# Two banks in turn for a layer's first groups, weight folding on four row groups with three buffers, and another order of tiles

## The chip, the cores and the metric

The kernel runs on one core of one Trainium2 chip. The metric is the device time of one execution in microseconds; of several executions the median is given. The engines are TensorE (PE in the profile, its weight loads PEld), VectorE (DVE), ScalarE (ACT), GpSimd (POOL) and SyncE (SP); all five take their instructions in order, each from its own queue, and wait for each other by semaphores. DMA transfers are issued here by SP and POOL, and each transfer's end is a semaphore event as well.

## The reference

A batch of 1024 images of 16 x 16 with 16 channels, in fp32, goes through four layers. Each computes `x = x + f(groupnorm(x))` with 8 groups of two channels.

```python
def _tt_matvec(vector, cores):          # layer 0: a 4096 x 4096 matrix as a train of three cores
    res = vector[:, None]
    for core in cores:
        r, o, i, k = core.shape
        res_t = res.reshape(bs, r, i, -1)
        new = jnp.einsum('roik,brix->bkox', core, res_t)
        ...

def update(x):                          # layers 1 and 3
    xt = jnp.transpose(x, (0, 3, 2, 1))
    pre = _alive(xt)                    # 3x3 maximum of channel 3 over 0.1
    y1 = _depthwise(xt, conv1_w, conv1_b)
    y2 = _depthwise(xt, conv2_w, conv2_b)
    p = jnp.concatenate([xt, y1, y2], axis=1)
    h = jax.nn.relu(p.reshape(B * W * Hh, 48) @ fc0_w.T + fc0_b)
    d = (h @ fc1_w.T + fc1_b).reshape(B, C, W, Hh)
    xn = (xt + d) * (pre & _alive(d)).astype(xn.dtype)
    ...

def _L2_conv_ref(x, filters, bias):     # layer 2: 3x3 convolution, 16 to 16 channels
    ...

x = x + _L0_conv_ref(_gn(x), ...)
x = x + _L1_conv_ref(_gn(x), ...)
x = x + _L2_conv_ref(_gn(x), ...)
x = x + _L3_conv_ref(_gn(x), ...)
```

## The kernel before, in words

**Data.** The batch is two chunks of 512 images (NB). The free dimension of nearly all tiles is the 512 images of a chunk; lines of an image stand on the 128 partitions. Two buffers, `XN[0]` and `XN[1]`, hold the chunk that is worked on and the one that is prepared.

**Layer 0 (`layer_train`).** The train of cores is multiplied out on the chip: `train_setup` computes G, the product of two cores (`gs`, eight groups of four matmuls for each half of the input, evacuated by ACT at L554 and sent to memory), and `build(u)` multiplies G with the third core to the weights of one unit: eight matmuls on four row groups of 32 partitions (L1009) into four PSUM banks of tag "w", four copies by ACT (L1014), and sums by DVE (`mix`, L1027). The 4096 x 4096 product itself is done by seven products in the manner of Strassen, over the two chunks as one of its dimensions. It has five phases with 16 units each; a unit of phase 0 has two products, of phase 1 five, and of the others seven, each product being four matmuls of 512 columns (L1086). PSUM for this layer has eight banks: three with tag "o" for products, four with tag "w" for builds, and a single one with tag "m" for everything else.

**What lies beside the products.** The order of every engine is written by hand: `run(layer, us, loads, (bg, lo, hi))` calls the main steps one by one and drops background steps between them, by the cost that each is given; a number alone in such a list is a pause. Phase 0 has as background, among others, the second chunk's input: `turn` transposes the input (four transposes into one bank at L829, one copy by ACT at L832 or L840, then a DMA), `spread` does the same with mean and deviation (`ptmr`), and `all_gs(1, "m")` computes the second half of G (L550, L554). The bank's tag is `tag[0]`, "m" in phase 0.

**The folds.** Layers 1 and 3 apply the Sobel filters by folding them into fc0: for each tap and pattern of lines, fc0's weights of 16 channels are combined with the filters' taps. `nca_weights(pre, room)` makes these steps for one of the two layers: `inputs`, `dense0`, `bias_lines`, `bias_rows`, `dense1`, `taps`, `order`, `xpats`, and the steps of `fold(n)`, 11 folds in each layer. All of them lie in scratch space in `XN[1]`, which is free at that time (`room`: one half for layer 1 and one for layer 3; `tmp(rows, line, lo, n)` is a piece of line `line` in it). Their input is `fs`, three kinds of rows by three taps, and `tp`, the taps in the order in which the fold wants them. A fold has three steps: `half(0)`, `half(1)` and `send`. A half is two matmuls with 96 rows and 36 columns of weights, of which 9 rows hold values and the others zeros, on two column groups of one bank (L382); `evac` copies the two results, one by ACT (L152) and one by DVE (L154), into one of the two buffers `fold_e`. `send` starts the DMAs from that buffer to memory on POOL's queue (L394), 160 in all. The buffers are used in turn, so a fold's copies wait for the sends of the fold two before it.

The folds run as the background of phase 1. `beside(make1, make3)` interleaves the lists of the two layers with pauses after each step:

```python
pause = [12, 8, 1, 1, 6, 6, 4, 4] + [1] * (len(xs) - 8)
return [z for x, y, t in zip(xs, ys, pause) for z in (x, 2.6, y, 2.6, t)]
```

**Layers 1 and 3 (`layer_nca`).** For each group of lines the kernel loads weights (`wq`), multiplies on four row groups (`ph`, L1451), applies relu on ACT into a tile `hid` (L1454), multiplies by fc1 on four column groups (L1304), and DVE and POOL finish: L1316 into `u`, the mask at L1353 (`u` times `mask`), the residual at L1354 (`res`), then a DMA to memory (`xf`, SP, L1356).

**Layer 2 (`layer_conv`)** begins with ACT's copies of border lines into `hx` (L1169), which the matmuls of L1190 read; L1181 multiplies the lines, ACT's L1229 takes them from PSUM. Beside it DVE (L596) and ACT (L614) compute sums and squares for the next norm, from lines that SP loads (L774).

**Where tiles lie.** Each stage opens a pool in SBUF and one in PSUM (`stage`), and a pool places its tags in the order in which they are first asked for. A tile that is placed where another stage's tile lay waits for that one's last reader or writer.

Of the kernel before, what the change touches and what calls it, by code (L numbers as in the profile page):

```python
# [18 lines left out]
B, S, C = 1024, 16, 16  # L19
# [84 lines left out]
def conv_preact_kernel(ctx: ExitStack, tc: tile.TileContext, a: dict, out: bass.AP):  # L104
# [34 lines left out]

    def bank(shape, tag, name):  # L140
        p, sizes = pool["ps"]
        return p.tile(shape, F32, tag=tag, name=name, bufs=sizes[tag])

    def psum(shape, name):
        return bank(shape, shared[0], name)
# [74 lines left out]
    def nca_weights(pre, room):  # L220
# [17 lines left out]
        fs = tmp(96, 5, 0, S * HID)  # L238
        tc3 = tmp(96, 2, 384, 96).rearrange("p (j k) -> p j k", k=3)
        tk = tmp(96, 9, 0, 32 * len(TERMS)).rearrange("p (n c) -> p n c", c=32)  # L240
        tp = tmp(96, 14, 0, 72 * len(TERMS)).rearrange("p (n f m) -> p n f m", f=2, m=36)
        pk = tmp(P, 10, 0, 833)
        fold_e = [tmp(P, 12, 0, 2 * NB), tmp(P, 3, 0, 2 * NB)]
        zero = tmp(32, 0, 256, HID)
        def inputs():
# [23 lines left out]
            V.memset(fs, 0.0)  # L269
# [49 lines left out]
        def taps():  # L319

            for n, terms in enumerate(TERMS):
                for s, kw in terms:
                    rows = slice(32 * s, 32 * s + 3)
                    V.tensor_copy(tk[rows, n], tc3[rows, :, kw])
            for s in range(3):
                for kh in range(3):
                    G.dma_start(
                        fs[32 * s + kh : 32 * s + kh + 1],
                        fz[s, 2 - kh : 18 - kh].rearrange("h k -> (h k)").unsqueeze(0),
                    )  # L330

        def order():

            for f in range(2):
                for k in range(3 - f):
                    for g in range(4):
# [5 lines left out]
                            tk[:, :, c0 : c0 + 12 * len(qs) - 11 : 12],  # L342
# [16 lines left out]
        def fold(n):  # L359

            steps = []
            for f in range(2):
# [13 lines left out]
                turn[0] ^= 1  # L376

                def half(a2, f=f, e=e):
                    pe = psum([P, NB], pre + "pe")
                    for hh in range(2):  # L380
                        h0 = NB * (2 * hh + a2)
                        T.matmul(  # L382
                            pe[64 * hh : 64 * hh + 36], tp[:, n, f], fs[:, h0 : h0 + NB],
                            start=True, stop=True,
                        )
                    for hh in range(2):
                        rows = slice(64 * hh, 64 * hh + 36)
                        evac(e[rows, NB * a2 : NB * a2 + NB], pe[rows])
# [12 lines left out]
                steps += [lambda half=half: half(0), lambda half=half: half(1), send]  # L401
# [84 lines left out]
    def train_setup(room):  # L486
# [84 lines left out]
        return [cores, sums] + all_gs(0, "w"), all_gs(1, "m")  # L571
# [674 lines left out]
    def layer_nca(X, n, l, L, xo=None):  # L1246
# [43 lines left out]
        def start():  # L1290
            st["m"] = work([P, 8, NB], "mask", "mask", BF16)
# [218 lines left out]
    def beside(xs, ys):  # L1510

        pause = [12, 8, 1, 1, 6, 6, 4, 4] + [1] * (len(xs) - 8)
# [4 lines left out]
    with ExitStack() as es:  # L1517
# [14 lines left out]
        tag[0] = "m"  # L1532
# [91 lines left out]
```

## Time and profile before

| | before |
|---|---|
| time, three runs | 3164.03, 3164.98, 3168.49 us; median 3164.98 us |
| span of the profiled run | 3163.8 us, mean granted TensorE clock 0.982 |
| TensorE | 3054.8 us busy, 13874 matmul records |
| VectorE | 1783.3 us busy |
| ScalarE | 1080.6 us busy |
| GpSimd | 673.2 us busy |
| layer 0's phase 0 | about 60 to 237 us |
| folds in phase 1 | first one at 299 us |

How to read it: a group's line names the line of the code, the engine and operation, and what is written and read; an "x4" behind a matmul's name counts records, and an fp32 matmul leaves two of them. `xn` in the names of the folds and of the input is the scratch space in `XN`. "Idle before" is the time the engine waited ahead of those instructions, with what ended the wait behind the arrow. Only waits of the engine that sets the end cost time.

### The profile page before, as it was taken

To read this page: it belongs to the slowest core of one execution; us is meant where nothing else is said; L and a number is where in the kernel's file an instruction comes from. 1 tells how busy PE (TensorE), PEld (TensorE's weight loads), DVE (VectorE), ACT (ScalarE), POOL (GpSimd) and SP (SyncE) were. 2 spreads that over 40 slices of the span, in tenths; PEclk is the share of its full clock that TensorE was granted. 3 is DMA by queue.
4 is the path that set the end of the run, shared out by engine and by line. 5 is a ranking of instruction groups with operands and counts; after the bars stand their busy time and mean duration, and the time that the engine had idled before them with its cause. 6 is when DMAs were issued, how large, how long until landed. Compare 5 with 4: busy or idle time off the path is not lost.

```text
span 3163.8 us, 37175 instructions
## 1 busy us (share of the span) xinstructions
PE 3054.8 (97%) x13874; PEld 1258.0 (40%) x13874; DVE 1783.3 (56%) x2374; ACT 1080.6 (34%) x1754; POOL 673.2 (21%) x714
## 2 busy tenths in 40 slices
PE   7899899999999999999999999999999999999996
PEld 4444333444444444444444433333333333333332
DVE  5245345755554555554555768657877747754222
ACT  4331121100000010000101166666665755655553
POOL 1116532200000000000000025435542224433221
PEclk8999999999999999999999999999999999999997
DMA  7535545443333433332222154445455764424444
GB/s 287 197 146 92 131 100 162 129 145 110 105 105 118 149 117 109 109 108 85 85 85 90 68 176 144 131 145 171 140 191 76 186 155 158 134 91 121 129 136 178
DMA packets 241826, 418.61 MB, mean 132 GB/s; under 512 B 37204, under 2 KB 91312, under 8 KB 238576
## 3 DMA queue, kind: packets, MB, share of 16 engines
q1 hardware_dynamic: 216160, 362.46, 34.6%
q0 software_dynamic: 24672, 53.49, 8.4%
q8 instruction: 110, 1.80, 0.2%
q14 instruction: 68, 0.56, 0.1%
q10 hardware_dynamic: 816, 0.30, 0.0%
HBM read 238.79 MB, written 165.60 MB: 128 GB/s over the span
## 4 chain that ended last, share of the span: by engine, by line
issue 49%; PE 30%; POOL 9%; DMA 3%; SPq 1%; DVE 1%; POOLq 0%; ACT 0%; DVEq 0%; ACTq 0%
PE ph L1451 11%; PE po L1086 9%; PE po L1304 4%; POOL u L1353 3%; POOL res L1354 3%; PE po L1181 2%; PE L_conv_pe L382 1%; POOL xf L1232 1%; DMA L_conv_wy<-xn 1%; SPq L949 1%; PE ptout L956 1%; PE pw L1009 1%; POOL L_conv_wy L394 0%; PE ptx L1363 0%; DMA xn<-xf 0%
## 5 line engine op out<-in xcount | busy, mean ns | idle before, releaser
L1086 PE MATMUL po<-xn,w 128*128 128x512 f32 x3584 | 1586.7, 598 | 4.6 <-DVE xn L900 4.6
L1086 PEld LDWEIGHTS po<-xn,w 128*128 128x128 f32 x3584 | 670.7, 191 | 854.0 <-issue 835.0
L1454 ACT ACTIVATE hid<-ph,pack 128x512 f32<-128x512 f32 x1024 | 653.9, 686 | 430.9 <-PE ph L1451 312.0
L1122 DVE TENSOR_TENSOR r<-r,po 128x512 f32<-128x512 f32 x576 | 378.3, 684 | 499.1 <-PE po L1086 476.4
L1353 POOL TENSOR_TENSOR u<-u,mask 128x512 f32<-128x512 f32 x128 | 203.1, 1587 | 1860.6 <-DMA nx<-xn 1272.7
L1451 PE MATMUL ph<-xn,wq 32*128 32x512 f32 x3664 | 575.1, 614 | 1.9 <-DMA wq<-L_conv_wy 1.9
L1014 ACT COPY w<-pw 128x512 f32<-128x512 f32 (+1 forms) x320 | 150.6, 557 | 1194.1 <-issue 971.3
L1451 PEld LDWEIGHTS ph<-xn,wq 32*128 32x128 f32 x3664 | 229.1, 185 | 264.1 <-issue 231.9
L1451 PE MATMUL ph<-xn,pack 32*128 32x512 f32 x1288 | 301.9, 631 | 2.3 <-ACT hid L1454 1.1
L1304 PE MATMUL po<-hid,pack 128*32 128x512 f32 x2048 | 284.3, 612 | 3.1 <-ACT hid L1454 2.7
L1027 DVE TENSOR_TENSOR w<-w 128x512 f32<-128x512 f32 x320 | 211.8, 687 | 116.8 <-ACT w L1014 116.3
L629 DVE TENSOR_TENSOR xn<-xn,m 128x1024 f32<-128x1024 f32 x160 | 225.8, 1460 | 44.6 <-ACT m L644 44.5
L1354 POOL TENSOR_TENSOR res<-res,u 128x512 f32<-128x512 f32 x128 | 212.5, 1660 | 16.6 <-DMA res<-xf 6.8
L1316 DVE SCALAR_TENSOR_TENSOR u<-po,pack,xn 128x512 f32<-128x512 f32 x128 | 95.9, 749 | 158.0 <-PE po L1304 153.3
L1181 PE MATMUL po<-xn,convw 128*128 128x512 f32 x368 | 167.2, 606 | 5.1 <-ACT conv L1229 5.1
L1451 PEld LDWEIGHTS ph<-xn,pack 32*128 32x128 f32 x1288 | 114.5, 187 | 97.4 <-issue 62.0
L1122 DVE TENSOR_TENSOR xn<-xn,po 128x512 f32<-128x512 f32 x96 | 64.4, 685 | 125.9 <-PE po L1086 125.8
L1304 PEld LDWEIGHTS po<-hid,pack 128*32 128x32 f32 x2048 | 42.9, 108 | 191.7 <-issue 136.1
L596 DVE TENSOR_TENSOR sq<-sq 128x1024 f32<-128x1024 f32 x78 | 106.9, 1371 | 13.1 <-ACT sq L614 10.8
L1181 PEld LDWEIGHTS po<-xn,convw 128*128 128x128 f32 x368 | 69.2, 193 | 103.4 <-issue 92.9
L394 POOL DMA_DIRECT2D L_conv_wy<-xn x160 | 89.0, 563 | 97.5 <-ACT xn L152 90.1
L596 DVE TENSOR_TENSOR s<-s,xn 128x1024 f32<-128x1024 f32 x60 | 86.3, 1439 | 9.6 <-DMA xn<-xf 8.1
(164 smaller groups left out, 1837.4 us busy)
## 6 DMA issues: line engine op xcount, KB each, us to landing
xf<-r SPq DMA_DIRECT2D x112, 512.0 KB, 3.8
xn<-xf SPq DMA_DIRECT2D x96, 512.0 KB, 4.9
r<-xf SPq DMA_DIRECT2D x80, 512.0 KB, 4.5
wq<-L_conv_wy SPq DMA_DIRECT2D x192, 192.0 KB, 2.8
res<-xf SPq DMA_DIRECT2D x128, 256.0 KB, 3.0
xf<-res SPq DMA_DIRECT2D x96, 256.0 KB, 2.0
res<-xr SPq DMA_DIRECT2D x256, 64.0 KB, 2.8
xf<-conv POOLq DMA_DIRECT2D x64, 256.0 KB, 5.9
```

The lines of the kernel that those rows point to most:

```text
L596: V.tensor_tensor(st["t"], st["t"], x, ALU.add)
L629: V.tensor_tensor(part, part, m().unsqueeze(1).broadcast_to([P, 2, NB]), op)
L1014: A.copy(w[:, k0:4, :, 32 * r : 32 * r + 32].rearrange("p k t (v o) -> p v (k t) o", v=2), pw[r],)
L1027: V.tensor_tensor(w[:, k], w[:, x], w[:, y], ALU.add if sign > 0 else ALU.subtract)
L1086: T.matmul(po, st["w", u][:, matrix, t], x, start=t == 0, stop=t == 3)
L1122: V.tensor_tensor(r[at], r[at], po, ALU.add if sign > 0 else ALU.subtract)
L1181: T.matmul(st["po", h][wh], conv["fw"][:, y], X[:, 16 * wh + h + y - 1], start=y == max(0, 1 - h), stop=y == min(2, S - h),)
L1304: T.matmul(po[32 * j : 32 * j + 32], nca["w1"][:, v], hid[j], start=v == 0, stop=v == 1)
L1353: G.tensor_tensor(u, u, st["m"][:, w2], ALU.mult)
L1354: G.tensor_tensor(r, r, u, ALU.add)
L1451: T.matmul(ph, w, x, start=k == 0, stop=k == len(tiles) - 1)
L1454: A.activation(h, ph, AF.Relu, bias=nca["bt"][:, r : r + 1])
```

## The change

It has four parts.

1. `bank` knows a tag "mw", which stands for "m" and "w" in turn. Phase 0's transposes and the second half of G use it, so that two groups in succession have two banks: the single "m" bank, and one of the four that the builds use.
2. The fold's rows are packed: `fs` holds 9 rows in each of four row groups, each with a quarter of the lines, where it held them among 96 rows. A fold is one step `make`: four matmuls with 9 rows and 36 columns of weights on four row groups, in two banks of tag "w", and four copies, all on ACT. For this the taps are copied to all four row groups (`tk4`, twelve more DMAs for each of the two layers), and `tp` has 128 partitions. There are three buffers `fold_e` instead of two. A fold has two steps instead of three, so the list of each layer has 8 + 2 x 11 steps.
3. In `beside` three pauses early in the list are longer.
4. `start` of `layer_nca` asks for a `hid` tile before the mask, in the first chunk's pool of layer 1 and in both of layer 3. So `hid` is the first tag of the pool, and the tiles lie elsewhere: before, the mask lay at byte 156192 of a partition and `hid` from 185888; now `hid` lies from 156192 to 172576 and the mask at 172576. Layer 2's first `hx` tile lies at 156192 in both.

All other lines are the same; their numbers move by 5 to 13.

```diff
--- before.py
+++ after.py
@@ -137,8 +137,13 @@
         p, sizes = pool["sb"]
         return p.tile(shape, dt, tag=tag, name=name, bufs=sizes[tag])
 
+    either = [0]
+
     def bank(shape, tag, name):
         p, sizes = pool["ps"]
+        if tag == "mw":
+            either[0] ^= 1
+            tag = "mw"[either[0]]
         return p.tile(shape, F32, tag=tag, name=name, bufs=sizes[tag])
 
     def psum(shape, name):
@@ -235,12 +240,14 @@
         fc0t, fcb = tmp(16, 1, 0, 3 * HID), tmp(48, 2, 0, 3 * HID)
         ind = tmp(48, 3, 0, 768).rearrange("p (s r) -> p s r", s=3)
 
-        fs = tmp(96, 5, 0, S * HID)
+        fs = tmp(P, 5, 0, NB)
+        tk4 = tmp(P, 6, 0, 32 * len(TERMS)).rearrange("p (n c) -> p n c", c=32)
+
         tc3 = tmp(96, 2, 384, 96).rearrange("p (j k) -> p j k", k=3)
         tk = tmp(96, 9, 0, 32 * len(TERMS)).rearrange("p (n c) -> p n c", c=32)
-        tp = tmp(96, 14, 0, 72 * len(TERMS)).rearrange("p (n f m) -> p n f m", f=2, m=36)
+        tp = tmp(P, 14, 0, 72 * len(TERMS)).rearrange("p (n f m) -> p n f m", f=2, m=36)
         pk = tmp(P, 10, 0, 833)
-        fold_e = [tmp(P, 12, 0, 2 * NB), tmp(P, 3, 0, 2 * NB)]
+        fold_e = [tmp(P, line, 0, 2 * NB) for line in (12, 7, 3)]
         zero = tmp(32, 0, 256, HID)
         def inputs():
             G.dma_start(fc0n, a[pre + "fc0_w"])
@@ -266,7 +273,7 @@
                         )
             V.memset(tk, 0.0)
             V.memset(tp, 0.0)
-            V.memset(fs, 0.0)
+            V.memset(tk4, 0.0)
             for s in range(3):
                 for base, step in ((s, 1), (15 - s, -1)):
                     G.affine_select(
@@ -323,10 +330,13 @@
                     rows = slice(32 * s, 32 * s + 3)
                     V.tensor_copy(tk[rows, n], tc3[rows, :, kw])
             for s in range(3):
+                for g in range(4):
+                    r0 = 32 * g + 3 * s
+                    G.dma_start(tk4[r0 : r0 + 3], tk[32 * s : 32 * s + 3])
                 for kh in range(3):
                     G.dma_start(
-                        fs[32 * s + kh : 32 * s + kh + 1],
-                        fz[s, 2 - kh : 18 - kh].rearrange("h k -> (h k)").unsqueeze(0),
+                        fs[3 * s + kh : 97 + 3 * s + kh : 32],
+                        fz[s, 2 - kh : 18 - kh].rearrange("(g h) k -> g (h k)", g=4),
                     )
 
         def order():
@@ -339,7 +349,7 @@
                         col = 12 * k + 4 * (qs[0] - 1) + g
                         G.tensor_copy(
                             tp[:, :, f, col : col + 4 * len(qs) - 3 : 4],
-                            tk[:, :, c0 : c0 + 12 * len(qs) - 11 : 12],
+                            tk4[:, :, c0 : c0 + 12 * len(qs) - 11 : 12],
                         )
             for n, pats in enumerate(TRIPLES):
                 for i, pat in enumerate(pats):
@@ -373,19 +383,19 @@
                 if not uses:
                     continue
                 e = fold_e[turn[0]]
-                turn[0] ^= 1
-
-                def half(a2, f=f, e=e):
-                    pe = psum([P, NB], pre + "pe")
-                    for hh in range(2):
-                        h0 = NB * (2 * hh + a2)
+                turn[0] = (turn[0] + 1) % 3
+
+                def make(f=f, e=e):
+                    pe = [bank([P, NB], "w", pre + "pe") for _ in range(2)]
+                    for g in range(4):
+                        rows = slice(64 * (g // 2), 64 * (g // 2) + 36)
                         T.matmul(
-                            pe[64 * hh : 64 * hh + 36], tp[:, n, f], fs[:, h0 : h0 + NB],
+                            pe[g % 2][rows], tp[32 * g : 32 * g + 9, n, f], fs[32 * g : 32 * g + 9],
                             start=True, stop=True,
                         )
-                    for hh in range(2):
-                        rows = slice(64 * hh, 64 * hh + 36)
-                        evac(e[rows, NB * a2 : NB * a2 + NB], pe[rows])
+                    for g in range(4):
+                        rows = slice(64 * (g // 2), 64 * (g // 2) + 36)
+                        A.copy(e[rows, NB * (g % 2) : NB * (g % 2) + NB], pe[g % 2][rows])
 
                 def send(e=e, uses=uses):
                     for k, s, v in uses:
@@ -398,7 +408,7 @@
                                 e[r0 : r0 + 12].rearrange("p (h k) -> p h k", h=8),
                             )
 
-                steps += [lambda half=half: half(0), lambda half=half: half(1), send]
+                steps += [make, send]
             return steps
 
         steps = [inputs, dense0, bias_lines, bias_rows, dense1, taps, order, xpats]
@@ -568,7 +578,7 @@
                 (1, lambda h=h, o=o: gs(h, ih, o, 4, tag)) for h in range(2) for o in range(2) for _ in range(2)
             ]
 
-        return [cores, sums] + all_gs(0, "w"), all_gs(1, "m")
+        return [cores, sums] + all_gs(0, "w"), all_gs(1, "mw")
 
 
 
@@ -1288,6 +1298,9 @@
             nc.sync.dma_start(r, tile_cw(xf[l][n], i))
 
         def start():
+            if n == 0 or l == 3:
+
+                work([P, NB], "hid", "hid")
             st["m"] = work([P, 8, NB], "mask", "mask", BF16)
             for m in range(AHEAD):
                 weights(m)
@@ -1509,7 +1522,7 @@
 
     def beside(xs, ys):
 
-        pause = [12, 8, 1, 1, 6, 6, 4, 4] + [1] * (len(xs) - 8)
+        pause = [12, 8, 1, 1, 6, 14, 10, 6] + [1] * (len(xs) - 8)
         return [z for x, y, t in zip(xs, ys, pause) for z in (x, 2.6, y, 2.6, t)]
 
     L1, make1 = nca_weights("L1_conv_", X1[:, 0:16])
@@ -1529,7 +1542,7 @@
         start, phases = layer_train()
         start()
         now(normed(0, 0, 1) + combined(0, True))
-        tag[0] = "m"
+        tag[0] = "mw"
         late = lines[0][10:] + lines[1][4:]
         loads, stat, lines, tail = input_steps(1, tag, 2, G)
         woven_in = [x for j in range(2) for i in range(4) for x in stat[j][i : i + 1] + lines[j][4 * i : 4 * i + 4]]
```

## The prediction, made before the changed kernel ran

> **What bounds the kernel now.** I read the page first: part 1, then part 2. The times are 3164.03 to 3168.49 us with 3164.98 as median, and the profiled run has a span of 3163.8 us at a granted clock of 0.982.
>
> ```profile
> PE 3054.8 (97%) x13874; PEld 1258.0 (40%) x13874; DVE 1783.3 (56%) x2374; ACT 1080.6 (34%) x1754; POOL 673.2 (21%) x714
> PE   7899899999999999999999999999999999999996
> PEclk8999999999999999999999999999999999999997
> ```
>
> TensorE is busy for 97% of the span. Nothing else comes near it, so an edit pays in two ways only: by fewer microseconds of matmul, or by less idle time of TensorE (109 us in all, a good part of it at the two ends). The slices (79.1 us each) that are not full at the start are the first, and then slices 2 and 5: layer 0's first phase and its second, which is where three of the four edits lie. Next I read the groups by line and shape; columns: busy us, mean ns of one, idle before it, and what ended that.
>
> ```profile
> L382 PE MATMUL L_conv_pe<-xn 96*36 96x512 f32 x176 | 47.3, 616 | 9.4 <-DVE xn L154 9.4
> L829 PE MATMUL ptin<-ident,xn 128*128 128x128 f32 x256 | 39.4, 287 | 15.7 <-ACT lines L840 13.2 <-ACT xn L832 2.6
> L550 PE MATMUL pg<-cores,xn 16*128 16x128 f32 x128 | 20.0, 315 | 3.0 <-ACT g L554 3.0
> L394 POOL DMA_DIRECT2D L_conv_wy<-xn x160 | 89.0, 563 | 97.5 <-ACT xn L152 90.1 <-issue 2.5 <-DMA L_conv_wy<-xn 2.2
> ```
>
> These are the folds (L382, with the sends of POOL at L394), the transposes of the input (L829) and the products of the train's cores (L550). The waits that stand against them are the single "m" bank's, and DVE's copy L154 for the folds. Last, the timeline of TensorE; columns: start, duration, what, number of records, and the idle time ahead. An fp32 matmul leaves two records, so x4 is two matmuls, and a 512-wide one takes 0.886 us.
>
> ```profile
> 65.30 0.60 PE L829 MATMUL ptin<-ident,xn 128*128 128x128 f32 x4
> 66.63 0.66 PE L829 MATMUL ptin<-ident,xn 128*128 128x128 f32 x4 [0.73 <-ACT lines L840]
> 67.12 1.88 PE L1086 MATMUL po<-xn,w 128*128 128x512 f32 x4
> 68.84 0.60 PE L829 MATMUL ptin<-ident,xn 128*128 128x128 f32 x4
> 69.28 1.88 PE L1086 MATMUL po<-xn,w 128*128 128x512 f32 x4
> ...
> 96.42 1.15 PE L550 MATMUL pg<-cores,xn 16*128 16x128 f32 x8 [0.72 <-ACT g L554]
> 97.50 3.68 PE L1086 MATMUL po<-xn,w 128*128 128x512 f32 x4
> ...
> 317.79 1.06 PE L382 MATMUL L_conv_pe<-xn 96*36 96x512 f32 x4
> 318.78 3.70 PE L1086 MATMUL po<-xn,w 128*128 128x512 f32 x8
> ...
> 344.65 1.06 PE L382 MATMUL L_conv_pe<-xn 96*36 96x512 f32 x4 [2.11 <-DVE xn L154]
> 345.63 1.98 PE L1086 MATMUL po<-xn,w 128*128 128x512 f32 x4
> 353.53 1.93 PE L382 MATMUL L_conv_pe<-xn 96*36 96x512 f32 x4 [5.91 <-DVE xn L154]
> 355.39 2.75 PE L1086 MATMUL po<-xn,w 128*128 128x512 f32 x4
> 358.07 1.15 PE L1009 MATMUL pw<-R,gq 32*128 32x256 f32 x16
> 359.15 1.05 PE L382 MATMUL L_conv_pe<-xn 96*36 96x512 f32 x4
> ```
>
> The reader is to see three things. Two groups on one bank directly after each other cost a wait of 0.7 us (66.63), which isn't there where products lie between (68.84). After each such pair of core products (96.42) the next two products take 3.68 us instead of 1.88. And a half of a fold holds TensorE for 0.99 us (317.79 to 318.78).
>
> **What the Trainium skill says.** "TensorE: Matmul & The Clock Gate", Part 3 (Packing small matmuls): matmuls in different row groups of the array run at once, measured as 3.07 times as fast for four with 32 rows. The trace agrees for L1009: eight matmuls of 256 columns on four row groups pass in 1.08 us (382.23 to 383.31), against 8 x 0.443 = 3.5 us one by one. Its Part 1 (The HAM clock gate) says that after an idle window of about 3.4 us TensorE runs at half clock for a while; the trace shows 1.93 instead of 1.06 us right after the 5.91 us of idle. "TensorEngine Tiling (Array Packing)", Gotcha 1 (PSUM Pressure): different row tiles can't use one PSUM bank at the same time. Nothing that I read in the trace shows this, and it bears on the new fold, where row groups 0 and 2 share a bank. "DMA: Bandwidth & Descriptors", Anatomy of one DMA: about 2.0 us fixed for each, which matters for the added copies of the taps.
>
> **The change part by part.**
>
> *Two banks for phase 0's small groups.* It removes the wait between two groups in succession. The waits of TensorE from 60 to 237 us on L829 and L550 are 10.5 + 2.6 + 3.0 = 16.1 us, 20 times. The visible wait is less than what a pair costs: a single transpose group costs 0.44 us (68.84 to 69.28), so a pair should cost 0.88, and the waiting one costs 1.82 (65.30 to 67.12): 0.94 for 0.73 seen. 16.1 x 0.94/0.73 = 20.7; I take 19.5, since the share differs. What remains: the second bank is now one of the four "w" banks that the builds use, and where the instruction order puts a group directly behind a build, it waits for ACT's L1014. There are four such places, 0.5 us each, +2; another +1 for groups whose wait ends only a little earlier. Sum -16 (bounds -13 to -19). The slow products behind L550 lose 1.7 us four times, some 7 us. If the short idle and the few busy rows of the pairs cause that, the wait's removal may end it or not; I take -2 (bounds 0 and -7). DVE and ACT copies of phase 0 move along with TensorE: DVE runs without a break from 215 to 249 us, but TensorE waits for none of it.
>
> *The fold on four row groups.* Before: 22 folds x 2 halves x 0.99 us = 43.6 us. After: 22 folds of four matmuls in four row groups, 512 wide, which the trace has no row for. If they overlap fully, 0.886 plus the change of tile mode of about 0.13 (seen at L1009 and at 2567.51, where eight logical matmuls on four row groups took 1.93 us) gives 1.05. Lower bound 0.95, upper bound 1.9 if the shared banks make two passes of it. I take 1.05: 22 x 1.05 = 23.1, so -20.5. The summed cost of the instructions that TensorE executes until the last build of phase 1 falls by 20.4 in the same reckoning.
>
> *Three buffers, other pauses.* TensorE's idle ahead of L382 was 9.4 us, in three waits (0.44, 2.11, 5.91 and some short ones). They came because POOL was still at its setup until 332.4, then sent 35 pieces in 19.46 us, and ACT's L152 waited for those with the two buffers full. The first fold comes a unit later now, and a third buffer stands ready: -9.4, and the slow stretch behind it (1.93 and 2.75 against 1.06 and 1.88) -1.8. Against that: POOL has 24 copies more, 24 x 0.5 us = 12 us of issue, and its setup for the last layer is ready at about the time when TensorE wants it: +1.5 (bounds 0 and 5). All four copies of a fold are on ACT now, 4 x 0.58 = 2.3 us and 0.2 to begin, and the folds use the builds' banks. In three places of the order a build follows only two matmuls (1.8 us) after the second fold of a pair: about 1 us each, +3. What stands behind a waiting build on TensorE is everything, as the queue is in order; that is why it is counted in full. A fourth fold waits for its buffer's sends, and with it ACT, up to 3 us, but eight or more matmuls (7 us) are between it and the next build, which hides it. DVE loses 30.6 us of copies, which nobody waited for.
>
> *Another order of tiles in layers 1 and 3.* The "hid" tile now lies where the mask lay. At layer 2's start ACT's first hx copy waited for POOL's last use of the mask (4.46 us at 2339.59), TensorE 4.68 behind it. That wait becomes one on matmuls long done. But at 2413.02 TensorE waits 5.08 us for ACT's L1229, and the chain there starts from DVE's statistics, whose DMA loads arrive at 2346.5 regardless; so what is gained first is waited later: 0 (bound -5). At the last boundary, 2.48 us of ACT and 0.90 us of TensorE vanish at 2825.66, but TensorE waits 3.27 us at 2832.87 for a load whose SP queue is unchanged: 0 (bound -1).
>
> **Sum:** -16 - 2 - 20.5 - 9.4 - 1.8 + 1.5 + 3 = -45.2; 3164.98 - 45.2 = 3120 us.
>
> **Rivals.** *The shared bank makes two passes of each fold*: 22 x 0.9 = 20 us come back: 3140. For it: the skill's sentence. Against it: nothing that I read in the trace. The same total comes if POOL's and ACT's new waits take 15 to 20 us. *More is gained*: the slow products after L550 are gone (-5 more) and layer 2's start keeps its 5 us: 3110. For it: the slow clock stands only beside those pairs. Against: DVE's fixed start in layer 2. *Slower*: the folds' matmuls don't overlap at all, 3.7 us each: 22 x 2.65 = 58 us more than I count, 3178; or ACT, blocked by a full buffer ahead of a build's copies, stops TensorE for 5 us at each of 11 pairs, 3175. Against it: L1009 overlaps, and the third buffer makes such blocks rarer. *No change*: the gain is waited away later, 3163. Against it: from 237 us to 1800 us TensorE waits for little outside these folds, so nothing downstream can soak it up.
>
> **How the numbers follow.** The likeliest case has 0.56, two passes (or stalls of that size) 0.17, more gained 0.19, slower 0.05, no change 0.03. The likeliest spreads by its bounds from 3112 to 3128; the range reaches over two passes and over more gained, 3105 to 3143. Faster 0.92, same 0.03, slower 0.05.
>
> **What would show it.** In the profile after: L829's and L550's idle falls from 18.7 to some 3 us, L550 is still followed by products at half speed (or isn't); the fold is one row of x176 records with 9 rows, and takes about 1.05 us up to the next product (1.9 would be the two passes); its idle is under 2 us; L1009 gets some 3 us of waits for ACT; in layer 2, the wait for hx goes and one for L1229 grows. A new wait of TensorE in 290 to 530 us above 10 us in all would make the prediction wrong.

## The result, and the profile after

The changed kernel takes 3131.5 us (median of four runs, 3127.2 to 3133.6), the kernel before, measured beside it, 3165.2; the ratio is 0.989 (0.9873 to 0.9907). Here and below, the brackets behind a time hold the fastest and the slowest run, those behind a ratio its 95% interval. The forecast was 3120 with a range of 3105 to 3143: faster, as forecast, but by 34 us instead of 45.

The page of the changed kernel, parts 1 and 2:

```profile
span 3128.5 us, 37206 instructions
...
PE 3025.4 (97%) x13874; PEld 1261.2 (40%) x13874; DVE 1747.8 (56%) x2330; ACT 1101.7 (35%) x1798; POOL 685.6 (22%) x738
...
PE   7999899999999999999999999999989999999996
```

TensorE lost 29 us of busy time, and it is still busy for 97%. Slice 2 is full now; slice 5, in the first half of phase 1, still isn't, and at three quarters (slice 30, layer 2) one has a gap that wasn't there. The groups by line and shape of the changed kernel (busy, mean ns of one, idle before it and what ended that; L392 is the fold, L839 the transposes, L560 the core products, L1019 the builds, L693 the mean for the norm of layer 2's second chunk) say which waits went and which came:

```profile
L1019 PE MATMUL pw<-R,gq 32*128 32x256 f32 x1024 | 76.7, 404 | 10.2 <-ACT xn L398 10.2
...
L839 PE MATMUL ptin<-ident,xn 128*128 128x128 f32 x256 | 38.2, 299 | 1.8 <-ACT w L1024 1.8
...
L392 PE MATMUL L_conv_pe<-xn 9*36 9x512 f32 x176 | 23.7, 609 | 0.0
...
L560 PE MATMUL pg<-cores,xn 16*128 16x128 f32 x128 | 19.4, 317 | 0.4 <-ACT w L1024 0.4
...
L693 PE MATMUL pmean<-s1s,gm_wc 128*128 128x512 f32 x4 | 3.2, 893 | 9.6 <-DVE s1s L614 9.6
```

The 18.7 us of idle time ahead of L829 and L550 became 2.2, and the 9.4 us ahead of L382 became nothing. In their place stand two single waits: 10.2 us of a build for the fold's copies, and 9.6 us of layer 2's mean for VectorE.

To see where each microsecond went, take the starts of the same matmuls in both traces (the first of a phase, a layer's chunk, and so on) and subtract. Both kernels do the same matmuls in each phase and layer, but for the folds in phase 1, so the stretches compare one to one (between the halves of a phase some background work can move: 13 of the 22 folds start in phase 1's first half before, 12 after). By its products phase 0 runs from 45.0 to 234.6 us in the kernel before, somewhat longer than the 60 to 237 us given above:

| stretch | before, us | after, us | difference |
|---|---|---|---|
| up to phase 0 | 45.0 | 46.3 | +1.3 |
| phase 0, first half of its products | 113.7 | 97.7 | -16.0 |
| phase 0, second half | 76.0 | 70.9 | -5.1 |
| phase 1, first half | 194.8 | 183.3 | -11.5 |
| phase 1, second half | 169.0 | 160.4 | -8.6 |
| phases 2 to 4 | 1223.4 | 1223.4 | 0.0 |
| layer 1, both chunks | 514.4 | 516.8 | +2.4 |
| layer 2, first chunk | 112.5 | 119.2 | +6.7 |
| layer 2, second chunk | 111.5 | 110.9 | -0.6 |
| layer 3, both chunks | 603.7 | 599.8 | -3.9 |

**Phase 0.** The timeline of TensorE in the changed kernel (start, duration, what, records; an idle time ahead in brackets):

```profile
65.91 1.04 PE L839 MATMUL ptin<-ident,xn 128*128 128x128 f32 x8
66.78 1.88 PE L1096 MATMUL po<-xn,w 128*128 128x512 f32 x4
...
94.92 2.05 PE L560 MATMUL pg<-cores,xn 16*128 16x128 f32 x16
96.89 1.98 PE L1096 MATMUL po<-xn,w 128*128 128x512 f32 x4
```

The pair of transposes takes 0.87 us up to the next product where it took 1.82, and the products behind a pair of core products take 1.98 us where they took 3.68. The waits account for most of the gain: over phase 0 TensorE stands idle for 4.6 us instead of 19.7.

**Phase 1.** The same view around the new wait:

```profile
349.71 1.06 PE L392 MATMUL L_conv_pe<-xn 9*36 9x512 f32 x8
350.71 3.70 PE L1096 MATMUL po<-xn,w 128*128 128x512 f32 x8
354.34 1.06 PE L392 MATMUL L_conv_pe<-xn 9*36 9x512 f32 x8
355.33 7.13 PE L1096 MATMUL po<-xn,w 128*128 128x512 f32 x16
362.40 0.70 PE L1019 MATMUL pw<-R,gq 32*128 32x256 f32 x4
373.30 2.55 PE L1019 MATMUL pw<-R,gq 32*128 32x256 f32 x12 [10.20 <-ACT xn L398]
375.78 3.78 PE L1096 MATMUL po<-xn,w 128*128 128x512 f32 x4
```

A whole fold takes 1.00 us (349.71 to 350.71) where two halves took 1.98. But the build at 362.40 does two of its eight matmuls and then waits, and 2.55 and 3.78 us behind the wait, instead of the rest of 1.15 and of 1.98, are the low clock (the granted clock is 0.50 from 373 to 380 us). ScalarE's timeline has the cause:

```profile
359.45 2.15 ACT L398 COPY xn<-L_conv_pe 36x512 f32<-36x512 f32 x4 [14.19 <-DMA L_conv_wy<-xn]
371.58 2.15 ACT L398 COPY xn<-L_conv_pe 36x512 f32<-36x512 f32 x4 [9.99 <-DMA L_conv_wy<-xn]
```

These are the copies of the folds at 349.71 and 354.34, the seventh and eighth. They wait for sends out of the buffers that they want: the first of them until 359.45, 8.7 us after its fold has ended (of the 14.19 us of idle time the rest is before that), the second for all of its 9.99 us. Until they are copied, those two folds hold PSUM banks that the build needs. The sends begin only at 349.11, as GpSimd's timeline shows:

```profile
269.32 1.99 POOL L335 DMA_DIRECT2D xn<-xn  x4 [28.01 <-DVE xn L331]
271.30 1.66 POOL L337 DMA_DIRECT2D xn<-L_conv_fz  x3
272.95 2.04 POOL L335 DMA_DIRECT2D xn<-xn  x4
274.99 1.64 POOL L337 DMA_DIRECT2D xn<-L_conv_fz  x3
...
294.62 3.79 POOL L350 COPY xn<-xn 128x18 f32<-128x18 f32 x20 [2.92 <-DMA xn<-L_conv_fz]
...
348.55 0.57 POOL L324 DMA_DIRECT2D L_conv_pk<-xn  x1 [4.26 <-DMA xn<-xn]
349.11 7.30 POOL L404 DMA_DIRECT2D L_conv_wy<-xn  x13
```

GpSimd waits 28 us for VectorE's taps (L331), and behind that wait stand the copies of the taps (L335) and, between them, the transfers that fill `fs` (L337), which don't need the taps. In the kernel before it filled `fs` while it waited, and had nothing to issue between the taps and its own copies:

```profile
261.91 8.61 POOL L327 DMA_DIRECT2D xn<-L_conv_fz  x18 [0.89 <-DMA L_conv_fz<-xn]
281.24 3.85 POOL L340 COPY xn<-xn 96x18 f32<-96x18 f32 x20 [10.71 <-DVE xn L324]
```

Against the first product of phase 1 (at 234.6 us before, at 214.8 after) the first send comes at 98.3 us in the kernel before and at 134.3 in the changed one: 36 us later, while the first fold comes 25.7 us later (64.7 and 90.4).

**Layer 2.** What TensorE waited for from 2290 to 2400 us in the changed kernel (total, times, longest):

```profile
PE pmean L693 <- DVE s1s L614: 9.6, 1, 9.6
PE po L1191 <- ACT conv L1239: 5.1, 1, 5.1
PE po L1200 <- ACT hx L1179: 0.5, 1, 0.5
```

The wait for hx fell from 4.68 to 0.5, as the change meant. The mean's matmul used to find its sum ready and now waits 9.6. VectorE builds the sum from 16 lines that SyncE loads, and it is the loads that are late. Each of the last eight lines is waited for:

```profile
2337.95 1.23 DVE L606 TENSOR_TENSOR s<-s,xn 128x1024 f32<-128x1024 f32 x1 [1.37 <-DMA xn<-xf]
2339.22 0.69 DVE L614 TENSOR_TENSOR s1s<-s 128x512 f32<-128x512 f32 x1
```

Counted from the chunk's first convolution matmul, VectorE's last step of the sum (L614) starts at 40.6 us instead of 35.2, and TensorE, which no longer waits for hx, asks for it at 31.7 instead of 37.2. Both halves make the wait: 5.5 us that TensorE comes earlier and 5.4 that the sum comes later, less 1.3 us by which the sum was early before, are the 9.6.

### The profile page after: what moved, and what is told of

The parts are those of the page before. It is cut to its first block, busy times and chain, and to the rows that moved or that the text cites. A ratio compares the mean times of both kernels' runs of the same rounds, so it can differ in the third digit from the quotient of the medians.

```text
span 3128.5 us, 37206 instructions
## 1 busy us (share of the span) xinstructions
PE 3025.4 (97%) x13874; PEld 1261.2 (40%) x13874; DVE 1747.8 (56%) x2330; ACT 1101.7 (35%) x1798; POOL 685.6 (22%) x738
## 4 chain that ended last, share of the span: by engine, by line
issue 50%; PE 26%; POOL 8%; DMA 1%; DVE 1%; SPq 1%; POOLq 0%; ACT 0%; DVEq 0%
PE ph L1464 11%; PE po L1096 6%; PE po L1317 4%; POOL u L1366 4%; POOL res L1367 4%; PE po L1191 2%; POOL xf L1242 1%; PE ptout L966 1%; SPq L959 1%; PE L_conv_pe L392 0%; PE pw L1019 0%; PE ptx L1376 0%; DMA xn<-xf 0%; PE po L1200 0%; PE pcnt L1356 0%
## 5 line engine op out<-in xcount | busy, mean ns | idle before, releaser
L1024 ACT COPY w<-pw 128x512 f32<-128x512 f32 (+1 forms) x320 | 150.6, 557 | 1189.5 <-issue 1003.4
L1464 PEld LDWEIGHTS ph<-xn,pack 32*128 32x128 f32 x1288 | 115.5, 188 | 95.5 <-issue 62.1
L1019 PE MATMUL pw<-R,gq 32*128 32x256 f32 (+1 forms) x1280 | 91.6, 386 | 12.6 <-ACT xn L398 10.2
```

The source lines that it names most:

```text
L1024: A.copy(w[:, k0:4, :, 32 * r : 32 * r + 32].rearrange("p k t (v o) -> p v (k t) o", v=2), pw[r],)
L1464: T.matmul(ph, w, x, start=k == 0, stop=k == len(tiles) - 1)
```

## The experiments

Three theories stood at the start. A: the two waits that came are what is missing from the forecast, one made by GpSimd's longer setup, the other by the new place of `hid`. B: the gain in phase 0 is partly the folds'. C: the new waits are the day's luck of the transfers. All runs below that are named "without part 4" leave the dummy `hid` tile out, since that turned out to be the better base.

**Part 1 alone**, in the kernel before:

```diff
-        return [cores, sums] + all_gs(0, "w"), all_gs(1, "m")
+        return [cores, sums] + all_gs(0, "w"), all_gs(1, "mw")
...
-        tag[0] = "m"
+        tag[0] = "mw"
```

> The kernel before with part 1 alone (phase 0's transposes and core products on two banks). Theory: the waits in phase 0 and the slow products behind the core products go, so phase 0 loses the 21 us that it lost in the changed kernel (113.7 + 76.0 us before to 97.7 + 70.9) and nothing else moves: about 3144 us. Rival: a part of those 21 us came from the folds' other steps that also move work of GpSimd and ScalarE in phase 0; then this gains under 15 us.

3142.4 us (3140.3 to 3144.2), ratio 0.9922 (0.9905 to 0.9938). Phase 0's halves take 99.6 and 70.9 us, so they take 19.1 less than before, and the folds' waits in phase 1 are as before (9.6 us). The gain of phase 0 belongs to part 1: theory B falls.

**Without part 4**, from the changed kernel:

```diff
-            if n == 0 or l == 3:
-
-                work([P, NB], "hid", "hid")
```

> The changed kernel without part 4 (hid's tile asked for where it was before). Theory: layer 2's start gets back its wait for hx (4.5 us) and loses the 9.6 us wait of the mean's matmul for VectorE, since the stores of the convolution start later and collide less with the loads for the statistics: its first chunk takes 112 to 113 us instead of 119, and the whole 3124 to 3128 us. Rival: the 9.6 us come from the loads' own speed in that one profile: the chunk stays near 119 us or the time rises by 2 to 4 us, to 3134.

3120.0 us (3118.6 to 3122.3), ratio 0.9854 (0.9839 to 0.9869), where the changed kernel has 0.989 (0.9873 to 0.9907): faster without part 4, and by more than the theory's 3124 to 3128. Layer 2's first chunk takes 112.4 us and waits 4.7 for hx again; the wait for the mean is gone. Of the 11.6 us between the two profiles 6.8 are this chunk's; most of the rest lies in phase 1's first half (2.2) and in layer 1 (1.7).

**Part 4 in layer 3 alone**:

```diff
-            if n == 0 or l == 3:
+            if l == 3:
```

> The changed kernel with part 4 in layer 3 alone. Theory: layer 2's first chunk is back at 112 to 113 us as without part 4, and the last boundary keeps what the order gives it there, which I put at 0 to 2 us (the wait of 0.9 us for hid becomes a longer one for the load behind it): 3122 to 3128 us. Rival: the 3.9 us that the last chunk lost belong to the order and are lost again without it, so this beats the kernel without part 4 by about 4 us.

3125.4 us (3123.4 to 3128.2). Layer 2's first chunk is at 112.4. Layer 3's last chunk takes 341.1 us, against 340.3 without part 4 and 340.9 with all of it: no gain that shows. The 3.9 us that this chunk lost against before aren't the order's. In the kernel with part 1 alone, where nothing of layer 3 is changed, it takes 338.3, in the next one 345.2. The whole is slower than without part 4 by stretches that the edit doesn't touch (in this profile phase 0 took 102.2 us in its first half, against 97.4, and phase 1 185.8 in its first half, against 181.1).

**The mean later**, in the changed kernel:

```diff
-        run(layer_conv(X0, 0), 108, load_wc(X1, xf[2][1]), (norm_lines(X1), 0.09, 1.04), by=0.07)
+        run(layer_conv(X0, 0), 108, load_wc(X1, xf[2][1]), (norm_lines(X1), 0.18, 1.04), by=0.07)
```

> The changed kernel with the steps of the next norm in layer 2's first chunk begun at 0.18 of it instead of 0.09, so that the mean's matmul stands some 10 us later in TensorE's order. Theory: TensorE no longer waits 9.6 us for VectorE's sum there, the chunk takes 107 to 111 us, the whole 3120 to 3124 us. Rival: the wait moves to later steps of that norm, since VectorE's squares begin only behind the mean: the chunk stays within 2 us of 119.

3122.8 us (3119.8 to 3127.6). The chunk takes 110.2 us; 1.7 us are left of the wait for the mean, and one of 3.5 us for the variance's sum has come. So most of the 9 us are a matter of when TensorE asks. In this profile layer 2's second chunk and layer 3's last took 2.3 and 4.3 us more than in the changed kernel, so a part may be paid later; the median is 8.7 us lower all the same.

**Without the first stores of layer 2**, in the changed kernel. It leaves out the convolution's additions to rows 0 to 3 of the first chunk.

```diff
-                waiting.append((rows_wc(xf[2][n], wh, h), r.unsqueeze(1)))
+                if n or h > 3:
+                    waiting.append((rows_wc(xf[2][n], wh, h), r.unsqueeze(1)))
```

> The changed kernel, with the convolution's additions of rows 0 to 3 of the first chunk left out of layer 2 (eight transfers of GpSimd less; those rows keep x alone). Theory: in the changed kernel these transfers start some 4 us earlier against TensorE's first convolution matmul than before, and stand in the way of the sixteen loads for VectorE's sums; without them the sixteen lines land in 22 to 28 us instead of 34, TensorE waits under 2 us for the mean and the chunk takes 108 to 110 us instead of 119. Rival: the loads are slow for another reason (where tiles lie, or the loads' own start): the wait stays over 6 us.

In its one run (3120.6 us) the chunk takes 106.4 us, the mean waits for nothing, and VectorE's last step of the sum starts 29.5 us after the chunk's first matmul instead of 40.6. Of the lines behind the first none is waited for:

```profile
2313.40 17.84 DVE L606 TENSOR_TENSOR s<-s,xn 128x1024 f32<-128x1024 f32 x14
```

The view of the transfers shows how the two kinds get in each other's way; its GB/s are the rate in 40 slices of 0.75 us from the chunk's start on (without the first stores: 0.775 us). The loads are 16 transfers of 512 KB on SyncE's queue, the stores transfers of 256 KB on GpSimd's that add `conv` to memory. The changed kernel:

```profile
GB/s 0 246 104 0 0 0 0 0 243 232 306 322 410 322 377 415 421 410 404 415 432 415 410 382 339 371 243 273 306 292 311 295 311 300 287 309 317 284 306 295
```

The kernel before, from its own start of the chunk:

```profile
GB/s 115 235 0 11 0 0 0 117 325 229 355 366 377 426 432 415 421 410 415 421 421 404 404 421 399 415 404 393 415 410 336 303 289 309 319 295 279 320 303 303
```

Without the first stores:

```profile
GB/s 0 214 124 0 0 0 0 0 307 217 317 359 423 407 418 423 418 418 423 423 407 391 412 407 423 412 407 391 423 407 412 412 412 407 402 407 101 0 0 0
```

As long as the loads are alone, some 400 to 430 GB/s pass, and without the first stores this goes on to the last line. Once the stores join them, it is mostly 280 to 320 for both. In the changed kernel this begins at the 25th figure (18 us into the chunk), before at the 31st (22.5 us). ScalarE, no longer held by hx, takes the first products out of PSUM at 13.2 us into the chunk instead of 17.4, so the stores start 4 us sooner, and the last loads land later by some 5 us. TensorE loses at the mean what it gained at hx, and these 5 us besides.

**The copies of the taps from SyncE's queue**, without part 4:

```diff
-                    G.dma_start(tk4[r0 : r0 + 3], tk[32 * s : 32 * s + 3])
+                    nc.sync.dma_start(tk4[r0 : r0 + 3], tk[32 * s : 32 * s + 3])
```

> The kernel without part 4, with the 24 added copies of the taps issued from SyncE's queue instead of GpSimd's. Theory: the folds' one long wait (9 us, the build's matmul for ScalarE's copies, which wait for a buffer whose sends stand on GpSimd behind its setup) is there because these copies take GpSimd 12 us and their landings some more; without them the setup ends 10 us or more earlier, the wait is under 2 us and the first half of phase 1 takes 170 to 173 us instead of 181: about 3110 us. Rival: the setup's end is set by the chain of transfers that wait for each other, whoever issues them, and the wait stays above 6 us: 3117 to 3121 us.

3130.9 us (3128.8 to 3135.3). GpSimd's first send comes 121.7 us into phase 1 instead of 134.2, and no build waits for a fold's copies. But now SyncE's queue stands still for the taps, and the builds wait 12.7 us for the loads of `gq` (the part of G that a build reads) behind them; the first half of phase 1 takes 191.7 us. The setup does end earlier by the 12 us of the copies, as the theory says, and its forecast of the time fails: a wait came on another queue. That no build waits for the folds' copies proves less than it seems, as these new waits, with the low clock behind them, also put the first fold back, from 90.4 us into the phase to 113.2.

**The first fold later**, without part 4, in two steps:

```diff
-        pause = [12, 8, 1, 1, 6, 14, 10, 6] + [1] * (len(xs) - 8)
+        pause = [12, 8, 1, 1, 6, 14, 10, 20] + [1] * (len(xs) - 8)     # later_first_fold
+        pause = [12, 8, 1, 1, 6, 14, 10, 42] + [0] * (len(xs) - 8)     # folds_at_327
```

> The kernel without part 4, with a pause of 20 instead of 6 between the last setup step and the first fold. Theory: the setup on GpSimd is done when the third pair of folds wants its buffers, the wait of 9 us is gone, the first half of phase 1 takes 170 to 173 us for what stands in it, and about 3110 us in all, unless the folds now stand closer together later. Rival: the folds make work for GpSimd (160 sends) faster than it issues them, so the wait comes back at a later pair with over 5 us: 3117 to 3121 us.

3128.0 us (3124.3 to 3131.6). Against the start of phase 1 the first fold moved by 5.2 us, and a wait of 5.8 us remained. The profile of the matmuls puts it down to `gq`, but the weight load just ahead of it names the folds' copies:

```profile
372.26 1.83 PEld L1019 LDWEIGHTS pw<-R,gq 32*128 32x128 f32 x12 [6.18 <-ACT xn L398]
```

The wait stands at the same pair of folds, the fourth (356.5 and 361.2 us), since the first send starts only at 347.5, when the setup ends. So the shift was too small. The rival was right that a wait of over 5 us stays; that GpSimd can't keep up with the folds isn't shown by it. The time lies outside both forecasts.

> The kernel without part 4, with the first fold some 22 us later (at about 327 us) and the folds' own pauses of 1 left out, so that they end where they did. In the kernel with a pause of 20 the seventh and eighth folds stood at 356.5 and 361.2 us and ScalarE's copies for them were free at 357.9 and 370.6; here they stand at about 366 and 370. Theory: sends that start at 348 us and take 0.56 us a piece are all that is waited for, so the wait at the build falls under 2 us, the first half of phase 1 takes 170 to 174 us and the whole about 3110 us. Rival: with the folds closer together the wait comes back in the second half of the list, or the transfers delay the loads of gq: 3117 to 3122 us.

3115.5 us (3109.7 to 3120.5), ratio 0.984 (0.9824 to 0.9856). No wait of a build is left, and the first half of phase 1 takes 168.5 us. The second half takes 164.5 instead of 160.4, as more folds stand in it: 333.0 for the phase against 341.5 without the edit.

**Two buffers**, without part 4:

```diff
-        fold_e = [tmp(P, line, 0, 2 * NB) for line in (12, 7, 3)]
+        fold_e = [tmp(P, line, 0, 2 * NB) for line in (12, 3)]
...
-                turn[0] = (turn[0] + 1) % 3
+                turn[0] = (turn[0] + 1) % 2
```

> The kernel without part 4, with two fold buffers for each layer instead of three. Theory: ScalarE's copies block one pair of folds earlier, at about 334 us instead of 350, while GpSimd's sends still begin at 349 us: the build at 341 us waits 10 to 13 us and one behind it some more, so the first half of phase 1 takes 4 to 12 us longer than without this edit, and 3124 to 3132 us. Rival: the third buffer does nothing, since the same sends have to be waited for anyway: within 2 us of 3120.

3142.2 us (3136.4 to 3145.4). The builds wait 28.1 us, in two waits, the longer 19.5; the first half of phase 1 takes 201.7 us, 20.6 more. The mechanism is the expected one, and its size twice what I wrote down: the third buffer is worth all of 20 us here, since it carries two more folds (one of each layer) across GpSimd's setup.

**The folds' copies on VectorE**, without part 4:

```diff
-                        A.copy(e[rows, NB * (g % 2) : NB * (g % 2) + NB], pe[g % 2][rows])
+                        V.tensor_copy(e[rows, NB * (g % 2) : NB * (g % 2) + NB], pe[g % 2][rows])
```

> The kernel without part 4, with the folds' four copies on VectorE instead of ScalarE. Theory: the build waits since the folds hold two of its four banks until they are copied, not since ScalarE is busy; so the build's matmul waits for VectorE's copies as long as before, 9 us or more, and VectorE's own additions of products stand behind the blocked copy too: 3120 to 3135 us. Rival: ScalarE's order is the cause; then TensorE no longer waits for a copy at the build: 3110 us.

3129.0 us (3121.6 to 3135.2). The build still waits for the copies, now VectorE's: 5.2 us at the longest, 6.4 in three. So the banks are what holds it, whoever copies. The wait is shorter than the 9 us that I expected, and the trace tells why: against the start of phase 1 the first send comes at 132.0 us here, where it came at 134.2, and the build comes at 148.8 instead of 147.5, which makes 3.5 of the 3.8 us. The second half of the phase takes 6.4 us more; by what isn't settled.

**The old pauses**, without part 4:

```diff
-        pause = [12, 8, 1, 1, 6, 14, 10, 6] + [1] * (len(xs) - 8)
+        pause = [12, 8, 1, 1, 6, 6, 4, 4] + [1] * (len(xs) - 8)
```

> The kernel without part 4, with the pauses of the kernel before (6, 4 and 4 instead of 14, 10 and 6). Theory: the folds begin some 15 us earlier while GpSimd's setup ends at most some us earlier, so the third buffer is used up long before the first sends, and the build waits 15 to 25 us instead of 9: 3126 to 3138 us. Rival: the setup moves along with its steps, and the wait stays near 9 us: 3118 to 3122 us.

3129.1 us, but from 3118.6 to 3132.8, and the profile is of the run of 3118.6. It has waits of 6.4 us at the folds and builds, none over 3.1; 4.0 of them are folds that wait for GpSimd's setup itself, and only 1.7 are builds that wait for the folds' copies, not the 15 to 25 of the theory. The first half of phase 1 takes 182.3 us all the same, 1.2 more than with the longer pauses, with 3.3 us less of waits but a lower granted clock (0.96 on average over this half, against 0.97). What the other three runs waited for isn't seen; whether the longer pauses help stays open.

**The rows ahead of the taps**, without part 4:

```diff
         def dense1():
+            for s in range(3):
+                for kh in range(3):
+                    G.dma_start(
+                        fs[3 * s + kh : 97 + 3 * s + kh : 32],
+                        fz[s, 2 - kh : 18 - kh].rearrange("(g h) k -> g (h k)", g=4),
+                    )
...
         def taps():
...
-                for kh in range(3):
-                    G.dma_start(
-                        fs[3 * s + kh : 97 + 3 * s + kh : 32],
-                        fz[s, 2 - kh : 18 - kh].rearrange("(g h) k -> g (h k)", g=4),
-                    )
```

> The kernel without part 4, with the eighteen transfers that fill fs issued two steps earlier, ahead of the copies of the taps, instead of between them. Theory: in the kernel before, GpSimd issued these 8.6 us while it waited for VectorE's taps; in the changed kernel they stand on its queue behind the added copies, which wait for those taps, so the setup ends later by the copies' 12 us and by these 8.6 us. Moved ahead they are hidden again: the first send comes 8 to 9 us earlier against the start of phase 1 (125 instead of 134 us), the wait at the build shrinks from 9 us to under 2, the first half of phase 1 takes 172 to 175 us, and the whole 3110 to 3114 us. Rival: the setup is held by the transfers that wait for each other's landing at its end, and the first send comes less than 3 us earlier: 3118 to 3122 us.

3106.1 us (3105.1 to 3112.9), ratio 0.9816 (0.9802 to 0.983): the fastest of all, with the same transfers. GpSimd's timeline in this kernel:

```profile
239.03 9.50 POOL L312 DMA_DIRECT2D xn<-L_conv_fz  x18 [0.86 <-DMA L_conv_fz<-xn]
266.25 11.86 POOL L341 DMA_DIRECT2D xn<-xn  x24 [17.73 <-DVE xn L337]
278.10 3.31 POOL L351 COPY xn<-xn 128x18 f32<-128x18 f32 x20
...
331.61 8.95 POOL L405 DMA_DIRECT2D L_conv_wy<-xn  x16
```

The 18 transfers are issued ahead of the wait for VectorE, and 11.86 us of copies are all that stands behind it. The first send comes 119.8 us into the phase, 14 us earlier, more than the 9 expected: in the changed kernel the 18 transfers between the copies took 9.9 us of GpSimd's time, not 8.6, and it then stood 2.9 us until they had landed (the wait at 294.62). And TensorE at the eighth fold and the build behind it:

```profile
351.26 1.06 PE L393 MATMUL L_conv_pe<-xn 9*36 9x512 f32 x8
352.26 7.13 PE L1097 MATMUL po<-xn,w 128*128 128x512 f32 x16
359.32 1.15 PE L1020 MATMUL pw<-R,gq 32*128 32x256 f32 x16
360.40 1.98 PE L1097 MATMUL po<-xn,w 128*128 128x512 f32 x4
```

No wait, no low clock (1.00 over the whole half); the first half of the phase takes 168.8 us, 12.3 less than without the edit, and the second its 160.4.

Of the theories A stands for both waits, and C falls. The wait at the build is there in each of the five profiles that keep the changed kernel's folds and pauses (9.0 to 13.0 us). The wait for the mean in full was seen in one profile, as no other run keeps the order in layer 1 with nothing else changed behind it; but all eleven profiles without that order have the chunk at 112.0 to 112.7 us, and two edits of what should cause it moved it to 110.2 and 106.4.

## Why the prediction was right and wrong

*Two banks*: forecast -16 and -2, measured -21.1 in phase 0, +1.3 ahead of it. (The terms written down, -19.5, +2 and +1, make -16.5.) The price of 0.94 us for a wait of 0.73, and the 2.2 us left of waits for ACT's L1024, came as worked out (+2 and +1 were allowed). The slow products after the core products, which I let go for 2 of 7 us, are gone in this trace, but the low clock isn't: over phase 0's first half the granted clock is 0.92 on average in both traces, and in the changed kernel slow matmuls stand at 78 to 83 us instead, behind a wait for `gq`. Slow products after the core products come back in others with the same phase 0: its first half took 95.5 to 102.5 us over thirteen profiles, so this term has a spread of its own, as wide as my bounds of 0 and 7.

*The fold on four row groups*: forecast 1.05 us each and -20.5; measured 1.00, where two halves took 1.98. The Trainium skill's "TensorEngine Tiling (Array Packing)", Gotcha 1 (PSUM Pressure), which says that different row tiles cannot access one PSUM bank at the same time, made me keep a rival of two passes, 1.9 us each. The trace has none of it, with row groups 0 and 2 in one bank but on different partitions of it. The speed-up in the sense of the skill's "TensorE: Matmul & The Clock Gate", Part 3 (Packing small matmuls), is 4 x 0.886 / 1.00 = 3.5 here, above the 3.07 that the page gives for four matmuls with 32 rows.

*Three buffers, other pauses*: this step failed. I wrote that the third buffer "stands ready" and took -9.4 and -1.8, and put 1.5 us against it for GpSimd's setup, "ready at about the time when TensorE wants it", and 3 for builds behind folds. The waits ahead of the folds did go, but ScalarE's blocked copies held a build for 10.2 us, and the low clock behind it and the rest make 14.4 us in all (183.3 in the changed kernel, 168.8 with the rows moved). I had priced the 24 added copies at their own 12 us and had seen neither that the filling of `fs` now stands behind VectorE's taps with them, nor that the setup's end has to be set against the *seventh* fold, the fourth of its layer, which wants that layer's first buffer again, and not against the first. (The landing of the copies, for which the prediction names 2.0 us, took 1.7 us in the median and wasn't what counted.) I said of the blocked fourth fold of a layer "up to 3 us", hidden by 7 us of matmuls: it was 8.7 from its fold's end on, and the one behind it, the other layer's fourth, added 9.99. The 3 us for builds behind folds were too much: where nothing blocks ScalarE, builds wait for no copy. What came is what I had named among the rivals: new waits of GpSimd and ScalarE (there 15 to 20 us), with ScalarE "blocked by a full buffer ahead of a build's copies". I had set that at 5 us for each of 11 pairs; it came at one pair, with 10.2. The sign that I had set for being wrong, a new wait of over 10 us between 290 and 530 us, came with it.

*Another order of tiles*: forecast 0, bound -5; measured +6.7 in layer 2's first chunk. I did see that the gain at hx would be waited away, and named VectorE's statistics behind the loads as the reason. But I looked for the loss at the wait for ScalarE's `conv`, which stayed at 5.1 us, where it was the mean's, and I held the loads' landing to be fixed ("regardless"). An earlier ScalarE makes earlier stores, and while these run beside the loads, the loads land later. That is why the case lay outside this term's bound, which allowed for a gain only. At the last boundary the forecast held: the wait for `hid` is gone, the next one for `xs` came with 2.65 and 3.23 us where one of 0.47 and one of 3.27 had been.

*The sum*: by the two profiles the gain is 35.3 us, 9.9 less than the 45.2 of the forecast. The third step cost 14.4 us instead of 4.5, so 9.9, and the fourth 6.7. Against these 16.6 stand 1.8 us that phase 0 gave beyond my 18 (with the 1.3 ahead of it), 2.8 in phase 1 (34.5 us in the last experiment, where nothing waits, instead of the 31.7 that I took ahead of the new waits) and 2.1 in the layers' other stretches, which nothing that I tried ties to the change. So the time came as near as it did because errors offset each other. The 3120.0 without part 4 equals the forecast by luck of the same kind, not because its steps were right.

## What to carry to other kernels

In this kernel an instruction added to a queue waited where it was put, and everything behind it too: what needs nothing from the awaited engine goes ahead of the wait (here worth 14 us, with no transfer more). A further buffer helps for as many rounds as it lasts until its consumer starts, so find when the consumer starts and count rounds up to there. And before an engine off the path is freed earlier, ask which transfers it will start earlier and what else is landing then.

## What the hardware showed that I had not expected

In layer 2 loads alone ran at some 400 to 430 GB/s, and loads mixed with transfers that add to memory mostly at 280 to 320 in all. TensorE's clock cost or gave several microseconds between profiles with the same matmuls in a stretch: phase 0's first half took 95.5 us at a mean granted clock of 0.94 with the rows ahead of the taps and 102.5 at 0.87 with the folds at 327 us, with 4.1 and 4.3 us of idle time; the last chunk of layer 3 took 338.3 (clock 0.95) to 345.2 (0.92) over all fourteen profiles; and in the profile with part 4 in layer 3 alone the fourth pair of core products took 3.78 us instead of 2.05 with no idle time right ahead of it. What decides where the clock falls isn't shown. So between two kernels of this kind a difference of 3 us in the whole says little, and a stretch without such places (phases 2 to 4, equal to 0.01 us in all fourteen) says much.
